# Dividing the feed-forward part between two neighbours

## The chip, the core and the metric

The kernel runs on one core of a Trainium2 chip, as one program. The time is device microseconds of one execution; the program takes 11845.06 us (median of 3 runs, 11842.54 to 11851.63). A core has five engines with instruction streams of their own: PE (TensorE, matmul), DVE (VectorE), ACT (ScalarE), POOL (GpSimd) and SP, which in this kernel issues all the transfers. Each executes its instructions in order; semaphores tie them together. Sixteen DMA engines move the data between HBM and the on-chip SBUF; matmuls write to PSUM, which has 8 banks of 128 x 512 float32.

## The reference

The input `x` is (8, 96, 64, 64). Layer 0 is a selective-scan block with a convolution, layer 1 attention without softmax and a feed-forward part with quantized products:

```python
xz = layernorm(group_norm(x)) @ in_proj_w.T + in_proj_b
xi, z = split(xz, 2)                       # 192 channels each
xi = silu(depthwise_conv3x3(xi) + conv_b)
xs = stack([xi by rows, xi by columns, both reversed])       # K = 4 directions, L = 4096
dts, Bs, Cs = split(einsum('bkdl,kcd->bkcl', xs, x_proj_w), [6, 22])
delta = softplus(einsum('bkrl,kdr->bkdl', dts, dt_proj_w) + dt_proj_b)
h[t] = exp(delta[t] * A) * h[t-1] + (delta[t] * u[t]) * B[t];  y[t] = h[t] . C[t]
y = layernorm(sum of the 4 directions + D * u) * silu(z)
x = x + y @ out_proj_w.T + out_proj_b
t = tokens(x)
t = t + linear_attention(layernorm(t))     # 6 heads, no softmax
t = t + ffn(layernorm(t))                  # 96 -> 384 -> 96
# ffn: operands rounded to 8 bits (5 exponent, 2 mantissa), sums to 16 bits, relu between
```

## The kernel before, in words

Two images form a pair; a loop runs over four pairs, and once more for the end of the last. Tensors are laid out with channels on the partitions and 512 positions (`F`) in a row, so an image has 8 chunks (`NCH`). For one pair the loop body does:

1. `back` of the pair before (sum of the directions, normalization, output projection, keys and values of the attention) together with `project` of the new pair (normalizations, input projection into the padded tiles `ybuf`).
2. `tail` of the pair before, the feed-forward part, together with `convolve` of the new pair.
3. `gates`: Silu over the three tiles `xi`, on ACT, 24 instructions (L354).
4. `prepare`: the scan's inputs.
5. `scan`: all four directions of the pair, in an order written out by hand.

`tail` works on 16 items, an item being a chunk of one image. An item is a generator of three parts: loads of `tf` (L830) and `ta` (L832), the attention's product `pa` (L834), the sum `t2` on DVE (L836), and the function `norm`: `ncp` on PE (L670), its square `nsq` on ACT (L672), `nvp` on PE (L674), Ln and Exp on ACT (`nrs`, L189 and L190), the product `tq` on DVE (L677); then three matmuls `pf1` (L843) with ACT and DVE behind each (`h16` and `hq`, L845 to L847); then three `pf2` (L851), `y16` on ACT and DVE (L855, L856), the sum `ot` on POOL (L858) and its store (L859). One step of the generator `tail` starts an item and advances the two items before it by a part, so 16 items take 18 steps.

`convolve` does 9 taps for the tiles 0 and 2 of `xi` on DVE (L342, L344) and those of tile 1 on PE (`pc`, L328), in 19 steps. `together(one, other, n, m)` lets the program text alternate: for each of `n` steps of `one` so many steps of `other` that `m` are reached at the end, and then the rest of both.

`prepare` loops over 2 orders of the positions, 8 chunks and 2 directions, 32 rounds. A round projects `xi` to `pt` (L392, PE), copies it to `S` (L396, ACT), stores B and C of it (`bs`, `cs`, L398), and for each of three tiles T: `pq` on PE (L404), Softplus to `delta` on ACT (L408), `du` on DVE (L412), and `delta` split into three bfloat16 parts `dp`, by ACT (L424), DVE (`rest`, L425), ACT (L426) and POOL (L427). Then `du` and `dp` are stored (L359, L362), `dp` to `dl`. In the second order POOL first copies three transposed tiles (`u`, L384). The tiles `S`, `delta`, `du` and `dp` have 3 buffers each.

Except in `scan`, the instructions of all engines are put in order by a scheduler of the framework, which takes a neighbour's instruction forward when it estimates that the one due still waits; transfers go through one queue, SP's. A transfer waits, by the built order, for the one eight before it. The ACT tables are in sets: Ln and Exp in one, Silu and Softplus in others. The function `table` keeps the instructions that need one in program order and loads the set with Ln and Exp where it is due (L180); the loads of the other sets are put in by the compiler.

Of the kernel before, what the change touches and what calls it, by code (L numbers as in the profile page):

```python
# [16 lines left out]
PSUM = bass.MemoryType.PSUM  # L17
# [34 lines left out]
def vss_attn_ffn(ctx: ExitStack, tc: tile.TileContext, a: dict):  # L52
# [119 lines left out]
    def half(T):  # L172
        return 1 if T == 2 else 0
# [188 lines left out]
                nc.sync.dma_start(dst(DI * b + 128, 64), src[64 * b : 64 * b + 64])  # L362


    def prepare(xi, us, dl, du, bs, cs_):
        with ExitStack() as st:
            tmp = st.enter_context(tc.tile_pool(name="p2", bufs=3))
            ps = st.enter_context(tc.tile_pool(name="p2ps", bufs=3, space=PSUM))
            pd = st.enter_context(tc.tile_pool(name="p2pd", bufs=4, space=PSUM))

            for T in range(3):
                spread(lambda o, n: us[o : o + n], T, xi[T])
# [2 lines left out]
            for o in range(2):  # L375
                for c in range(NCH):
                    cs = bass.ts(c, F)
# [11 lines left out]
                    for k in (o, o + 2):  # L389
                        pt = ps.tile([128, F], F32, name="pt")  # L390
                        for T in range(3):
                            nc.tensor.matmul(  # L392
                                pt[:76], xw[:, k, T], u[T], start=(T == 0), stop=(T == 2)
                            )
                        S = tmp.tile([128, F], F32, name="S")
                        nc.scalar.activation(S[:76], pt[:76], AF.Copy)  # L396
                        for v, r in ((bs, 0), (cs_, 32)):
                            nc.sync.dma_start(  # L398
                                v[k, 2 * c : 2 * c + 2].rearrange("j p t -> p j t"),
                                S[r : r + 32].rearrange("p (j t) -> p j t", j=2),  # L400
                            )
                        for T in range(3):
                            pq = pd.tile([128, F], F32, name="pq")
                            nc.tensor.matmul(  # L404
                                pq, dtw[64:76, k, T], S[64:76], start=True, stop=True
                            )
                            d = tmp.tile([128, F], F32, name="delta")
                            table("softplus", lambda: nc.scalar.activation(  # L408
                                d, pq, AF.Softplus, bias=dtb[:, k, half(T) : half(T) + 1]
                            ))  # L410
                            q = tmp.tile([128, F], F32, name="du")
                            nc.vector.tensor_tensor(q, d, u[T], ALU.mult)  # L412
                            j = slice(c * F // TC, (c + 1) * F // TC)
                            spread(
                                lambda o, n: duv[k, j, o : o + n].rearrange("j p t -> p j t"),
                                T, q.rearrange("p (j t) -> p j t", t=TC),
                            )

                            dp = tmp.tile([128, F // TC, 3, TC], BF16, name="dp")
                            rest = tmp.tile([128, F], F32, name="rest")  # L420
                            d, rest = [
                                t.rearrange("p (j t) -> p j t", t=TC) for t in (d, rest)
                            ]
                            nc.scalar.activation(dp[:, :, 0], d, AF.Copy)  # L424
                            nc.vector.tensor_tensor(rest, d, dp[:, :, 0], ALU.subtract)  # L425
                            nc.scalar.activation(dp[:, :, 1], rest, AF.Copy)  # L426
                            nc.gpsimd.tensor_tensor(dp[:, :, 2], rest, dp[:, :, 1], ALU.subtract)  # L427
                            spread(
                                lambda o, n: dlv[k, j, :, o : o + n]
                                .rearrange("j a p t -> p (j a) t"),  # L430
                                T, dp.rearrange("p j a t -> p (j a) t"),
                            )


    def scan(dl, du, bs, cs_, ys):
# [431 lines left out]
                going = [g for g in going if next(g, 0) is None]  # L867
                yield

    def together(one, other, n, m):  # L870

        done = 0
        for i in range(n):
            next(one, None)
            while done * n < (i + 1) * m:
                next(other, None)
                done += 1
        for g in (one, other):
            for _ in g:
                pass  # L880

    old = {}
    for pair in range(npair + 1):

        new = {}
# [9 lines left out]
        none = iter(())  # L895
        with ExitStack() as pads, ExitStack() as xis:
            if new:

                yp = pads.enter_context(tc.tile_pool(name="yp", bufs=1, side="right"))
                ybuf = [yp.tile([128, (HH + 2) ** 2], F32, name=f"y{T}") for T in range(3)]  # L900
            with ExitStack() as st:
                def pool(name, bufs, **kw):
                    return st.enter_context(tc.tile_pool(name=name, bufs=bufs, **kw))
                one = other = none
                if old:
                    one = back(
                        pair - 1, old["ys"], old["us"], old["zs"], old["t1"], old["tn"],
                        pool("bk", 2), pool("bky", 1, space=PSUM), pool("bkc", 2, space=PSUM),
                        pool("bkm", 1, space=PSUM), pool("bkp", 2, space=PSUM),
                    )  # L910
                if new:
                    other = project(
                        pair, new["zs"], ybuf, pool("p1", 1, side="right"),
                        pool("p1t", 2, side="right"), pool("p1ps", 2 if old else 6, space=PSUM),
                    )
                together(one, other, 16 if old else 1, 34)
            if pair == 0:
                decay_weights()
            if new:
                xp = xis.enter_context(tc.tile_pool(name="xip", bufs=1))  # L920
                xi = [xp.tile([128, L], F32, name=f"xi{T}") for T in range(3)]
            with ExitStack() as st:
                one = other = none
                if old:
                    one = tail(
                        pair - 1, old["t1"], old["tn"], pool("tt", 3), pool("tps", 6, space=PSUM)
                    )
                if new:
                    other = convolve(
                        xi, ybuf, pool("p1c", 1, side="right"), pool("p1cp", 2, space=PSUM)  # L930
                    )
                together(one, other, 18 if old else 1, 19)
            pads.close()
            if new:
                gates(xi)
                prepare(xi, new["us"], new["dl"], new["du"], new["bs"], new["cs"])
        if new:
            scan(new["dl"], new["du"], new["bs"], new["cs"], new["ys"])
        old = new
# [114 lines left out]
```

## Time and profile before

| what | value |
|---|---|
| median of 3 runs | 11845.06 us |
| the profiled execution, its own time | 11820.4 us |
| its span, first to last instruction | 11818.4 us |
| mean granted PE clock | 0.816 |
| busiest engine, DVE | 8756.4 us, 74% |
| bytes moved | 2092.92 MB, mean 177 GB/s |
| `tail` and `convolve` together, second pair | 2980 to about 3162 us |
| gates, second pair | 3162.3 to 3179.9 us |
| `prepare`, second pair, first `delta` to last `dp` | 3182.6 to 3503 us |
| `tail` alone, after the last pair | 11636 to 11818 us |

Times in the profile are microseconds from the first instruction. A group is an engine's instructions of one line; `out<-in` are the tiles by their names in the program. A window gives each engine's busy time between two moments. In a timeline, the bracket behind an instruction is the idle time of its engine just before it and what ended it. The granted clock is the share of PE's full clock. Busy time of PE is modelled from pipelined matmuls.

### The profile page before, as it was taken

The page shows a single profiled execution, that of the slowest core. Times are in us where ns is not written, and L with a number is a line of the kernel's source. Part 1 is how long each engine was busy: PE and PEld are TensorE (multiplying, and loading weights), DVE is VectorE, ACT ScalarE, POOL GpSimd, SP SyncE. Part 2 cuts the span into 40 slices and gives each one's busy share as a digit, 9 for nine tenths or more (in the row PEclk, how much of TensorE's full clock was granted, in tenths as well). Part 3 has the DMA queues.
Part 4 walks back from the last instruction along what each step waited for, and adds up shares of the span by engine and source line. Part 5 has one row for each costly group of instructions (what it writes and reads, how often), then busy time and mean ns, then how long its engine had stood idle before and what let it go on. Part 6 is the DMA issues. An engine that isn't in the chain of part 4 may idle for free. (4 is left out here: it accounts for less than half of the span.)

```text
span 11818.4 us, 387513 instructions
## 1 busy us (share of the span) xinstructions
PE 8675.0 (73%) x170112; PEld 5662.7 (48%) x170112; DVE 8756.4 (74%) x6465; ACT 6900.1 (58%) x12176; POOL 7986.7 (68%) x2770
## 2 busy tenths in 40 slices
PE   7856666779877666667986666667898666667787
PEld 2245555544225555554422555555442355555542
DVE  5489999963549999995355999999454699999922
ACT  3556666644456666664455666666445566666623
POOL 0489999960249999994025999999313699999910
PEclk8678888879768888888976888888896788888896
DMA  2988888875398888886459888888646988888862
GB/s 79 215 198 201 198 203 201 198 160 134 97 215 195 203 201 200 204 195 149 120 125 209 197 202 199 197 199 199 148 99 156 203 199 199 200 198 200 193 132 63
DMA packets 1655919, 2092.92 MB, mean 177 GB/s; under 512 B 962179, under 2 KB 1307348, under 8 KB 1651412
## 3 DMA queue, kind: packets, MB, share of 16 engines
q1 hardware_dynamic: 1654228, 2068.13, 75.4%
q8 instruction: 1335, 21.87, 0.9%
q14 instruction: 356, 2.92, 0.1%
HBM read 1604.17 MB, written 463.54 MB: 175 GB/s over the span
## 5 line engine op out<-in xcount | busy, mean ns | idle before, releaser
L588 DVE TENSOR_TENSOR_SCAN h<-da,dbu 128x774 f32<-128x774 f32 x4096 | 7028.4, 1760 | 646.5 <-ACT da L577 443.1
L552 POOL TENSOR_TENSOR dbu<-dut,bc 128x1536 f32<-128x1536 f32 x2048 | 7083.1, 3506 | 578.1 <-ACT dbu L549 478.7
L577 ACT ACTIVATE da<-da 128x768 f32<-128x768 f32 x4092 | 3254.2, 797 | 2155.9 <-PE da L570 2117.6
L606 PE MATMUL yp<-h,cw 128*32 128x48 f32 x131072 | 3145.2, 246 | 1126.0 <-issue 1110.7
L570 PE MATMUL da<-dm,aw 128*128 128x128 bf16 x24576 | 2502.0, 251 | 1447.2 <-DVE h L588 1098.1
L606 PEld LDWEIGHTS yp<-h,cw 128*32 128x32 f32 x131072 | 2548.9, 155 | 1673.2 <-issue 1408.7
L570 PEld LDWEIGHTS <-aw 128*128 128x128 bf16 x24576 | 1844.5, 111 | 1774.5 <-issue 1452.5
L506 ACT ACTIVATE cw<-bc,blk 128x512 f32<-128x512 f32 x2048 | 1472.8, 720 | 297.9 <-DMA bc<-cs 216.2
L745 POOL TENSOR_TENSOR yk<-yk 128x768 f32<-128x768 f32 x64 | 115.8, 1809 | 1268.2 <-DMA yk<-ys 1010.6
L427 POOL TENSOR_TENSOR dp<-rest,dp 128x512 bf16<-128x512 f32 x384 | 458.1, 1194 | 707.3 <-ACT dp L426 691.6
L425 DVE TENSOR_TENSOR rest<-delta,dp 128x512 f32<-128x512 f32 x384 | 301.1, 785 | 628.2 <-ACT dp L424 628.2
L404 PE MATMUL pq<-S,dtw 12*128 12x512 f32 x768 | 594.8, 882 | 140.2 <-ACT delta L408 75.3
L614 ACT ACTIVATE yev<-yp 128x384 f32<-128x384 f32 x1024 | 503.4, 492 | 243.1 <-PE yp L606 240.6
L858 POOL TENSOR_TENSOR ot<-t,y 96x512 f32<-96x512 f32 x64 | 128.1, 2002 | 612.0 <-DVE y L856 593.7
L786 DVE SCALAR_TENSOR_TENSOR g<-yc,c_onw,yrs 96x512 f32<-96x512 f32 x128 | 89.9, 742 | 483.2 <-ACT yrs L190 483.2
L404 PEld LDWEIGHTS pq<-S,dtw 12*128 12x128 f32 x768 | 162.4, 250 | 566.0 <-ACT delta L408 179.1
L426 ACT ACTIVATE dp<-rest 128x512 bf16<-128x512 f32 x384 | 241.6, 630 | 327.3 <-DVE rest L425 327.3
L672 ACT ACTIVATE nsq<-ncp 96x512 f32<-96x512 f32 x128 | 75.8, 592 | 572.8 <-PE ncp L670 559.6
L549 ACT COPY dbu<-h 128x12 f32<-128x12 f32 x1984 | 407.1, 205 | 0.0
L758 PEld LDWEIGHTS py<-ident,yk 128*24 128x24 f32 x8192 | 231.6, 108 | 241.7 <-issue 182.6
L758 PE MATMUL py<-ident,yk 128*24 128x128 f32 x8192 | 319.1, 290 | 31.5 <-DVE yk L744 25.7
L384 POOL COPY u<-xi 128x512 f32<-128x512 f32 x96 | 109.3, 1156 | 327.6 <-ACT xi L354 296.6
(136 smaller groups left out, 6684.3 us busy)
## 6 DMA issues: line engine op xcount, KB each, us to landing
dut<-du SPq DMA_DIRECT2D x1024, 768.0 KB
dm<-dl SPq DMA_DIRECT2D x512, 576.0 KB
dl<-dp SPq DMA_DIRECT2D x256, 384.0 KB
dm<-dl SPq DMA_DIRECT2D x512, 192.0 KB
ys<-yev SPq DMA_DIRECT2D x1024, 96.0 KB
du<-du SPq DMA_DIRECT2D x256, 256.0 KB
bc<-bs SPq DMA_DIRECT2D x512, 128.0 KB
bc<-cs SPq DMA_DIRECT2D x512, 128.0 KB
```

Of the source, the lines that this page charges most:

```text
L404: nc.tensor.matmul(pq, dtw[64:76, k, T], S[64:76], start=True, stop=True)
L425: nc.vector.tensor_tensor(rest, d, dp[:, :, 0], ALU.subtract)
L427: nc.gpsimd.tensor_tensor(dp[:, :, 2], rest, dp[:, :, 1], ALU.subtract)
L506: nc.scalar.activation(cw[i % 2][:, :, :, m, :].rearrange("p z j t -> p (z j) t"), bc[i][:, 1].rearrange("p z (j t) -> p (z j) t", j=NB), ...
L549: nc.scalar.copy(start, segs(hs[s - 1][:, :, r])[:, :, :, 1 if back else TC])
L552: nc.gpsimd.tensor_tensor(segs(t)[:, :, :, 1:], dut[g // 2][:, NI * (r % 2) : NI * (r % 2) + NI, :].unsqueeze(1) .to_broadcast([128, 2, NI ...
L570: nc.tensor.matmul(e[:, i], aw[k, r][:, i, z, :], dm[s][:, NI * r + i, :], start=True, stop=True,)
L577: nc.scalar.activation(e, e, AF.Exp)
L588: nc.vector.tensor_tensor_scan(hs[s][:, w, r][:, d], da[p % 3][:, o : o + W6][:, d], dbu[4 * s + r][:, w][:, d], 0.0, ALU.mult, ALU.add,)
L606: nc.tensor.matmul(y[32 * q : 32 * q + 32, 2 * NE * i : 2 * NE * i + 2 * NE] .rearrange("p (j r i) -> p i j r", j=2, r=NR), w[:, z, :, t], ...
L614: nc.scalar.activation(yev[s][:, :, o : o + 8, :].rearrange("p j i e -> p i j e"), y[:, 0 : 16 * NE].rearrange("p (i j e) -> p i j e", j=2 ...
L758: nc.tensor.matmul(o, yk[:, k, 4 * g + e, NE * j : NE * j + NE], ident, start=False, stop=(k + j == 4),)
```

## The change

`together` gets an argument `rest`: with False it stops after `n` steps of `one` and only finishes `other`. `prepare` becomes a generator that yields after each of its 32 rounds. Feed-forward steps 1 to 7 stay beside the 19 steps of the convolution; then the padded tiles are given back and the gates follow; the other 11 steps alternate with the first 24 rounds of `prepare`, and its last 8 rounds follow. The PSUM banks are divided anew: `tail` has 4 (8 after the last pair) where it had 6, `pt` 2 where it had 3, `pq` 2 where it had 4 (4 in the first pair, which has no `tail` beside it).

```diff
-    def prepare(xi, us, dl, du, bs, cs_):
+    def prepare(beside, xi, us, dl, du, bs, cs_):
         with ExitStack() as st:
             tmp = st.enter_context(tc.tile_pool(name="p2", bufs=3))
-            ps = st.enter_context(tc.tile_pool(name="p2ps", bufs=3, space=PSUM))
-            pd = st.enter_context(tc.tile_pool(name="p2pd", bufs=4, space=PSUM))
+            ps = st.enter_context(tc.tile_pool(name="p2ps", bufs=2, space=PSUM))
+            pd = st.enter_context(tc.tile_pool(name="p2pd", bufs=2 if beside else 4, space=PSUM))
...
                                 T, dp.rearrange("p j a t -> p (j a) t"),
                             )
+                        yield
...
-    def together(one, other, n, m):
+    def together(one, other, n, m, rest=True):
...
-        for g in (one, other):
+        for g in (one, other) if rest else (other,):
             for _ in g:
                 pass
...
                     one = tail(
-                        pair - 1, old["t1"], old["tn"], pool("tt", 3), pool("tps", 6, space=PSUM)
+                        pair - 1, old["t1"], old["tn"],
+                        st.enter_context(tc.tile_pool(name="tt", bufs=3)),
+                        st.enter_context(tc.tile_pool(name="tps", bufs=4 if new else 8, space=PSUM)),
                     )
                 if new:
-                    other = convolve(
-                        xi, ybuf, pool("p1c", 1, side="right"), pool("p1cp", 2, space=PSUM)
-                    )
-                together(one, other, 18 if old else 1, 19)
-            pads.close()
-            if new:
-                gates(xi)
-                prepare(xi, new["us"], new["dl"], new["du"], new["bs"], new["cs"])
+
+                    with ExitStack() as sc:
+                        other = convolve(
+                            xi, ybuf, sc.enter_context(tc.tile_pool(name="p1c", bufs=1, side="right")),
+                            sc.enter_context(tc.tile_pool(name="p1cp", bufs=2, space=PSUM)),
+                        )
+                        together(one, other, 7, 19, rest=False)
+                    pads.close()
+                    gates(xi)
+                    other = prepare(
+                        bool(old), xi, new["us"], new["dl"], new["du"], new["bs"], new["cs"]
+                    )
+                together(one, other if new else none, 11 if old else 1, 24)
```

## The prediction

> **What bounds the kernel now.** I read the page first, then the stretch between two scans in windows, then the chain inside two of these windows, then the transfers. No engine is full over the span:
>
> ```profile
> PE 8675.0 (73%) x170112; PEld 5662.7 (48%) x170112; DVE 8756.4 (74%) x6465; ACT 6900.1 (58%) x12176; POOL 7986.7 (68%) x2770
> ```
>
> The change leaves the scans alone, so the stretch between two of them is what counts. The windows, for the second pair of images (columns: window, its length, PE, PEld, DVE, ACT, POOL busy with instruction counts, granted clock, DMA share, GB/s):
>
> ```profile
> 2980.00:3099.00 119.00, 103.05 (x247) 39.93 (x245) 116.05 (x121) 44.62 (x77) 31.60 (x13) 0.92 0.20 58
> 3099.00:3162.00 63.00, 46.61 (x68) 13.07 (x68) 22.25 (x53) 22.51 (x39) 6.67 (x6) 0.53 0.12 35
> 3162.00:3183.00 21.00, 14.87 (x30) 4.77 (x30) 3.03 (x9) 20.78 (x35) 6.43 (x7) 0.82 0.25 94
> 3183.00:3343.00 160.00, 155.21 (x199) 40.29 (x198) 64.72 (x95) 95.01 (x160) 57.72 (x49) 0.61 1.00 228
> 3343.00:3502.00 159.00, 116.89 (x164) 30.92 (x162) 78.47 (x102) 92.93 (x159) 77.35 (x67) 0.67 0.98 215
> ```
>
> Four stages stand there. Convolution beside the feed-forward part is bound by DVE (116 of 119 us). Then 63 us of feed-forward alone, with no engine full and the DMA at 0.12. Then the gates on ACT (20.78 of 21). Then `prepare`, 319 us, bound by the DMA (1.00 and 0.98). The third and fourth pairs show the same lengths within 3 us. The 63 us are a chain, one step of 10.9 us after the other, as ACT in the timeline shows (start, length, what, idle time before it and who ended it):
>
> ```profile
> 3147.72 0.59 ACT L672 ACTIVATE nsq<-ncp 96x512 f32<-96x512 f32 x1 [3.90 <-PE ncp L670]
> 3150.43 0.68 ACT L189 ACTIVATE nrs<-nvp,eps 96x512 f32<-96x512 f32 x1 [2.11 <-PE nvp L674]
> 3151.14 0.63 ACT L190 ACTIVATE nrs<-nrs 96x512 f32<-96x512 f32 x1
> 3151.76 0.59 ACT L855 ACTIVATE y<-pf 96x512 f16<-96x512 f32 x1
> 3152.96 1.58 ACT L845 ACTIVATE h<-pf 128x512 f16<-128x512 f32 x3 [0.60 <-PE pf L843]
> ```
>
> In `prepare` ACT runs one third of a (direction, chunk) round about every 3.3 us (320 us for 96 of them):
>
> ```profile
> 3234.26 0.63 ACT L424 ACTIVATE dp<-delta 128x512 bf16<-128x512 f32 x1 [0.20 <-DMA dl<-dp]
> 3235.65 0.63 ACT L426 ACTIVATE dp<-rest 128x512 bf16<-128x512 f32 x1 [0.76 <-DVE rest L425]
> 3236.18 0.67 ACT L408 ACTIVATE delta<-pq,c_dtb 128x512 f32<-128x512 f32 x1
> ```
>
> The first of the three waits for a store to land and free a buffer, so the DMA paces it. Two more rows: the transfers of 3200 to 3400, and PE inside `prepare`.
>
> ```profile
> q1 hardware_dynamic: 134826, 43.95, 100.5%
> ```
>
> ```profile
> 3250.00:3350.00 100.00, 100.00 (x119) 26.15 (x119) 41.96 (x63) 62.37 (x105) 36.70 (x32) 0.55 1.01 220
> ```
>
> The DMA is full at 220 GB/s, and PE shows busy throughout as well, but at a clock of 0.55.
>
> **The gain: 71 us in each of three pairs.** In the changed kernel's built order of DVE (a list without times) only feed-forward items 0 to 6 lie among the convolution's instructions. Before, a DVE period is 10.94 us (the `y` starts at 3060.54 and 3071.49), of which three convolution passes of 2.27 are 6.8, so an item costs 4.13. The convolution alone is 32 x 2.27 + 5.6 (four first passes) = 78.2; seven items add 29. So it ends at 2980 + 107 = 3087, against 3098.9 before, and the gates no longer wait for the rest of the feed-forward part. 16 to 17 us of gates remain behind it, to 3104; then ACT does item 7's `nsq`, waits for its `nvp` (2.0), does Ln and Exp (1.3) and loads the table of Softplus (1.3): about 7 us. First `delta` at 3111 instead of 3182.6. Bounds: 60, if the convolution ends no earlier than before (3098.9 + 17 + 7 = 3123), and 76, if item 7 hides under the gates. I take 71, the counted order.
>
> **What `prepare` pays.** Nine whole items (7 to 15) and the end of item 6 move in.
>
> DMA: in the built order of SP five `ta` loads, four `tf` loads and ten `out` stores now stand among `prepare`'s transfers, 19 x 192 KB = 3.74 MB; the other loads go ahead of it. At 220 GB/s that is 17 us; at the rate of the feed-forward part (9.05 MB took 16.9% of 182 us) 12.7. DMA is the bound here, so nothing hides it: 15.
>
> ACT: the order gives one feed-forward step per 24/11 rounds, 6.5 thirds, 21.8 us at today's pace. ACT needs at least 1.39 + 0.53 + 0.57 + 0.2 (its share of `S`) = 2.7 a third, 17.6 in all. A step adds nsq 0.59, Ln 0.68, Exp 0.63, three h 1.57, y 0.59 = 4.1 and two table loads, of which the order has 17 more per pair:
>
> ```profile
> 3162.33 1.28 ACT L354 ACT_TABLE_LOAD   x1
> 3163.63 0.72 ACT L354 ACTIVATE xi<-xi,c_convb 128x512 f32<-128x512 f32 x1
> ```
>
> From load to next instruction 1.30. Sum 17.6 + 4.1 + 2.6 = 24.3, less some 1.5 that fall into the 0.76 waits for `rest`: 22.8, against 23.2 that the DMA now needs (21.8 + 15/11). ACT is 98% full, so each wait of a feed-forward instruction costs. In the chain above ACT waits 3.90 + 2.11 + 0.60 = 6.6 a step for PE. If all showed, nine items cost 59; none, if `prepare`'s matmuls that the order puts between always cover them. I take 25: three instructions of `prepare` stand between most of these links, but not all.
>
> The Trainium skill ("ScalarE: Activation LUTs", What ACT_TABLE_LOAD costs, and its rules) speaks against this edit: finish one table set before switching, at about 2.66 us a switch, a drain included. The row above shows 1.3 and no drain. By the page the 17 switches are 45 us instead of 22 and ACT, not the DMA, would be the bound, with a sum about 23 us a pair worse.
>
> SP: `prepare`'s stores keep their order but for two places, where 14 and 7 small transfers stand in a row, among them `tf` loads that wait for PE's `pa` and a `ta` load that waits for DVE's `t2`; the stores `du` and `dl` queue behind, and with them `dp` buffers and ACT. Bounds 0 and one round of stores each (10.4, what ACT waited once for a `cs` store): 0 to 21. I take 2, since in the built order a transfer waits only for the one eight before it, so several are always under way. None of these edits can gain, as the DMA is full before.
>
> DVE gets 9 x 4.1 = 37 on 143 of 319 us, POOL nine `ot` at 1.15 to 3.14, so 10 to 28 on 135: both have room. An `ot` that waits for `y` holds the `dp` queued behind it; that is in ACT's bounds. PSUM: the feed-forward part has 4 banks instead of 6, `pq` 2 instead of 4, `pt` 2 instead of 3. Two `pq` are 6.6 us of ACT's pace, and the first stage is bound by DVE: 0, with ACT's 59 as cover for more. In the first pair only `pt` changes, 0 to 5 us. The last pair has 8 banks, but its order on PE, DVE and ACT is that of before: 0.
>
> **Sum.** 71 - 15 - 25 - 2 = 29 a pair, 87 in three. The profiled execution took 11820.4 (span 11818.4): 11733. The median is 24.7 above it: 11845 - 87 = 11758.
>
> **Rivals.**
> *It is hidden whole.* Only the transfers are paid: 71 - 17 = 54 a pair, 162 in all, 11683. For it: ACT, DVE and POOL are 59%, 45% and 42% busy in `prepare`. Against it: ACT's in-order sum above.
>
> *PE becomes the bound (slower).* At the low clock `pt` and `pq` take 0.925 us a record (3.70 for 4), 11.1 a round, which is more than the 10 us the DMA gives it; an item adds 1.91 + 1.99 + 2.02 + 1.44 + 1.49 = 8.9 (`pa`, `ncp`, `nvp`, `pf` twice, from the last pair, where the clock is 0.50), nine 80. Up to 3422, where the feed-forward part ends, PE has about 26 us left: 54, with the waits of 25 79, and if the waits also use up the slack 105. It turns slower at 71. Worst: 3 x (105 - 71) = 102, 11947. For it: 100 us at full occupancy without a rise of the clock. Against: the clock was 1.00 while the convolution ran beside the same items, and it reaches 0.86 for a few us whenever PE lags. The skill ("TensorE: Matmul & The Clock Gate", Part 1) says a window of 3.4 us without idling gives the full clock; by it this rival falls, since PE would need half the time. The row at 0.55 contradicts it.
>
> *No difference.* Costs of 63 to 79 a pair leave 11821 to 11869.
>
> **How the numbers follow.** Under 0.2% (24 us) this kernel's measurement can hardly be told from no change. Forecast (costs 25 to 63 a pair, 11707 to 11821): 0.50. Hidden: 0.15. No difference: 0.10. Slower, mostly by PE: 0.25. So faster 0.65, same 0.10, slower 0.25. The range leaves out a twentieth below the hidden case and some 0.15 above: 11675 to 11910; the faster cases alone span 11675 to 11821.
>
> **What the profile would show.** Right: the gates start near 3088 and the first `delta` near 3111; the window of feed-forward alone is gone; `prepare` lasts 355 to 365 us, DMA at 0.90 or more; ACT 250 us busy in it with 17 more table loads. Hidden: 335 us, DMA 0.98. PE: a clock near 0.5 with PE busy all through and the DMA under 0.85, `prepare` above 390. Wrong in the first step: the convolution ends after 3099.

## The result, and the profile after

The changed kernel takes 11842.4 us (median of 20 runs, 11819.98 to 11890.16), the kernel before on the same chip 11843.8 us (20 runs, 11793.85 to 11881.49). The ratio is 1.0008 with a 95% interval of 0.9996 to 1.0019: no difference that can be measured. 87 us of gain were forecast.

The two profiled executions have spans of 11818.4 and 11851.0 us. The stretches between two scans are 36 us longer in the second, all the rest 4 us shorter. The interval of the 20 runs leaves room for some 22 us of loss only, so a part of the 36 belongs to these two executions or is made up where these stretches do not show it; which, is not known. I cut the stretches by single instructions: the convolution's first tap, the table load ahead of the first `delta`, the end of the last `dp`, the scan's first instruction (us, for the three pairs that have a feed-forward part beside them):

| | before | after | forecast |
|---|---|---|---|
| convolution | 118.8, 118.3, 118.8 | 102.4, 102.4, 102.6 | 107 |
| first tap to first `delta`'s table | 201.2, 201.7, 201.3 | 118.6, 118.7, 118.8 | 71 less |
| `prepare` | 320.7, 321.6, 324.1 | 420.4, 420.3, 420.4 | 42 more |
| last `dp` to scan | 31.6, 31.8, 32.2 | 28.6, 28.3, 28.4 | the same |
| whole stretch | 553.5, 555.1, 557.6 | 567.6, 567.3, 567.6 | 29 less |

So the beginning gained more than forecast, 83 us a pair, and `prepare` lost 98 instead of 42. The first line of the page, and the windows of the second pair (columns as before: PE, PEld, DVE, ACT, POOL busy, granted clock, DMA share, GB/s), for convolution, gates and three parts of `prepare`:

```profile
PE 8636.7 (73%) x170112; PEld 5659.1 (48%) x170112; DVE 8794.6 (74%) x6465; ACT 6951.4 (59%) x12227; POOL 7975.4 (67%) x2770
```

```profile
2981.00:3084.00 103.00, 97.76 (x231) 39.77 (x231) 101.92 (x93) 35.48 (x61) 17.55 (x9) 0.93 0.17 50
3084.00:3100.00 16.00, 9.34 (x17) 2.94 (x16) 3.72 (x9) 15.94 (x28) 6.02 (x6) 0.82 0.38 152
3101.00:3261.00 160.00, 132.33 (x210) 37.87 (x209) 68.59 (x111) 94.67 (x155) 48.17 (x38) 0.71 0.78 179
3261.00:3390.00 129.00, 99.18 (x155) 27.89 (x153) 61.23 (x91) 76.84 (x129) 46.45 (x39) 0.70 0.73 160
3390.00:3521.00 131.00, 90.56 (x112) 22.32 (x112) 66.83 (x77) 67.61 (x115) 64.64 (x51) 0.60 0.88 195
```

The stage of feed-forward alone (63 us at a DMA share of 0.12) is gone. But `prepare` lost its bound: the DMA, 1.00 before, is at 0.78 and 0.73 while items run, and no other engine took its place. ACT is busy 59% of these 289 us, DVE 45%, POOL 33%. The transfers of 3200 to 3400, and PE in the window in which it was full before:

```profile
q1 hardware_dynamic: 93267, 33.00, 74.5%
```

```profile
3250.00:3350.00 100.00, 78.97 (x129) 22.42 (x128) 49.45 (x78) 64.33 (x106) 36.57 (x30) 0.74 0.81 176
```

33.0 MB where there were 43.95. PE stands at 79 of 100 us at a clock of 0.74, up from 0.55: the rival with PE as the bound wanted the opposite, a low clock with PE full. What is there instead is waiting. ACT, across the largest hole (start, length, what, the idle time before it and its releaser):

```profile
3220.66 0.63 ACT L426 ACTIVATE dp<-rest 128x512 bf16<-128x512 f32 x1 [0.76 <-DVE rest L425]
3221.19 0.57 ACT L396 ACTIVATE S<-pt 76x512 f32<-76x512 f32 x1
3233.31 0.59 ACT L673 ACTIVATE nsq<-ncp 96x512 f32<-96x512 f32 x1 [11.54 <-PE ncp L671]
3236.01 0.68 ACT L189 ACTIVATE nrs<-nvp,eps 96x512 f32<-96x512 f32 x1 [2.11 <-PE nvp L675]
```

The lines of DVE and SP for the same moment:

```profile
3219.93 0.69 DVE L425 TENSOR_TENSOR rest<-delta,dp 128x512 f32<-128x512 f32 x1 [1.81 <-ACT dp L424]
3230.51 0.68 DVE L837 TENSOR_TENSOR t<-ta,pa 96x512 f32<-96x512 f32 x1 [9.89 <-DMA ta<-t]
```

```profile
3224.33 1.44 SPq L362 DMA_DIRECT2D dl<-dp  x2
3225.82 0.85 SPq L860 DMA_DIRECT2D out_dram<-ot  x1
3226.72 0.93 SPq L833 DMA_DIRECT2D ta<-t  x1
...
3233.52 0.38 SPq L831 DMA_DIRECT2D tf<-tn  x1
3240.11 0.98 SPq L359 DMA_DIRECT2D du<-du  x2
```

Read from the last fence up: the load of `ta` stands in SP's queue behind the stores of a round, and is issued at 3226.72. `t2` on DVE (L837) waits 9.89 us for it; `ncp`, `nsq` and all that stands behind them on ACT and DVE wait too, though it belongs to `prepare`; so from 3225.8 to 3240.1 no `du` or `dl` is issued, and the DMA has little to move. The waits of ACT over 3101 to 3390 (sum, times, longest) say how much of this there is:

```profile
ACT dp L426 <- DVE rest L425: 40.4, 42, 1.8
ACT nsq L673 <- PE ncp L671: 30.0, 5, 11.5
ACT y L856 <- PE pf L852: 17.5, 6, 4.5
ACT delta L408 <- PE pq L404: 8.9, 11, 2.7
```

One loss in `prepare` has nothing to do with the feed-forward steps. Two memsets of the scan's tile `cw`, 6.9 us each, have moved. In the kernel before, both follow the last `dp` of `prepare`:

```profile
3501.98 1.15 POOL L427 TENSOR_TENSOR dp<-rest,dp 128x512 bf16<-128x512 f32 x1 [1.29 <-ACT dp L426]
3510.49 6.88 DVE L451 MEMSET cw<- 128x8192 f32 x1 [9.25 <-issue]
```

In the changed kernel, and in every run below that has feed-forward steps beside `prepare`, the one on POOL starts 13 to 54 us before the end of the last `dp`, and the one on DVE stands ahead of a late `rest` (here the last one), for which ACT waits:

```profile
3512.51 6.88 DVE L452 MEMSET cw<- 128x8192 f32 x1 [1.66 <-issue]
3519.32 0.62 DVE L425 TENSOR_TENSOR rest<-delta,dp 128x512 f32<-128x512 f32 x1
3519.98 0.63 ACT L426 ACTIVATE dp<-rest 128x512 bf16<-128x512 f32 x1 [8.39 <-DVE rest L425]
```

So the last round of `prepare` takes 17.3 us on ACT instead of 10.0, in all three pairs; of these 7 us only some 3 come back between the last `dp` and the scan. What the memset on POOL costs is not to be read from the trace, and no run moved either back.

### The profile page after: what moved, and what is told of

It reads as the page before. It is cut to its first block, busy times and chain, and to the rows that moved or that the text cites. A ratio compares the mean times of both kernels' runs of the same rounds, so it can differ in the third digit from the quotient of the medians.

```text
span 11851.0 us, 387228 instructions
## 1 busy us (share of the span) xinstructions
PE 8636.7 (73%) x170112; PEld 5659.1 (48%) x170112; DVE 8794.6 (74%) x6465; ACT 6951.4 (59%) x12227; POOL 7975.4 (67%) x2770
## 5 line engine op out<-in xcount | busy, mean ns | idle before, releaser
L859 POOL TENSOR_TENSOR ot<-t,y 96x512 f32<-96x512 f32 x64 | 100.6, 1572 | 523.9 <-DVE y L857 443.9
L550 ACT COPY dbu<-h 128x12 f32<-128x12 f32 x1984 | 407.3, 205 | 0.0
L384 POOL COPY u<-xi 128x512 f32<-128x512 f32 x96 | 112.1, 1182 | 332.7 <-ACT xi L354 298.0
```

The lines of the kernel that those rows point to most:

```text
L550: nc.scalar.copy(start, segs(hs[s - 1][:, :, r])[:, :, :, 1 if back else TC])
```

## The experiments

Each is told with the length of its `prepare` (before: mean 322.1, after: 420.4). Ratios are to the kernel before on the same chip. Runs without an interval are single executions and are read by their stages.

**First: four suspected costs, one by one.**

The loads ahead:

```diff
-            tns = [tmp.tile([DIM + 1, F], F32, name=f"tf{i}", bufs=1) for i in range(4)]
+            tns = [tmp.tile([DIM + 1, F], F32, name=f"tf{i}", bufs=1) for i in range(10)]
-                ta = tmp.tile([DIM, F], F32, name="ta")
+                ta = tmp.tile([DIM, F], F32, name="ta", bufs=10)
```

> The changed kernel with 10 buffers each for `ta` and `tf` instead of 3 and 4, so that all loads of the feed-forward part are issued before the stores of `prepare`; SP then has a regular order. Theory of the late loads: two holes in the DMA of `prepare` (from 3225 and from 3347 us, about 20 us each) vanish and `prepare` shrinks from 420 to about 380 us per pair, the whole kernel to about 11725. Theory of the in-order ACT (table loads and waits for PE): `prepare` stays above 410 and the kernel within 30 us of the changed one. Theory of the banks: no change either.

`prepare` 400.4, 395.2, 395.0: 23.5 us less, 11805.8 us, ratio 0.9957 (0.9943 to 0.9971), 0.4% faster than the kernel before. The late loads were a real cost, more than ten times what the forecast had. But 75 us remain.

No switches of tables (Ln and Exp of the feed-forward part replaced by Copy, so its outputs are not the reference's):

```diff
-        rsqrt(rs, vp[:DIM])
+        nc.scalar.activation(rs, vp[:DIM], AF.Copy)
+        nc.scalar.activation(rs, rs, AF.Copy)
```

> The changed kernel, with Ln and Exp of the feed-forward part replaced by two copies on ACT (its normalization is left out, so the output differs); no table switch is left in `prepare`, and the order of the table instructions is free there. Theory of the tables: the 18 loads of 1.28 us in `prepare` cost 23 us or more, so `prepare` falls from 420 to 395 or less. Theory of the late loads: ACT is not what fills the stage, `prepare` falls by less than 10, the two holes stay.

404.5, 403.6, 401.4: 17.2 us less. That is no clean price of the switches: without the order that the tables impose, the scheduler also put the items elsewhere (in the second pair no item's `nsq` stands between 3144 and 3237 us), and the late loads are still there. The Trainium skill ("ScalarE: Activation LUTs", What ACT_TABLE_LOAD costs) has about 2.66 us a switch, a drain of about 1.38 included, which would be 45 us for 17. In the rows of this case the load takes 1.28 us, the next instruction starts 1.30 us after it does, and no drain shows.

Fewer PSUM banks alone, in the kernel before (`pt` 2, `pq` 2):

```diff
-            ps = st.enter_context(tc.tile_pool(name="p2ps", bufs=3, space=PSUM))
-            pd = st.enter_context(tc.tile_pool(name="p2pd", bufs=4, space=PSUM))
+            ps = st.enter_context(tc.tile_pool(name="p2ps", bufs=2, space=PSUM))
+            pd = st.enter_context(tc.tile_pool(name="p2pd", bufs=2, space=PSUM))
```

> The kernel before with the PSUM banks of `prepare` cut as in the change (`pt` 2 instead of 3, `pq` 2 instead of 4), nothing moved. Theory of the banks: a good part of the 100 us shows here, `prepare` goes from 321 to over 340 us. The two other theories: 321 to 326, as the stores pace it.

330.2, 328.7, 332.7: 8.4 us, with nothing beside it.

Ten steps beside the convolution and eight beside `prepare`:

```diff
-                        together(one, other, 7, 19, rest=False)
+                        together(one, other, 10, 19, rest=False)
-                together(one, other if new else none, 11 if old else 1, 24)
+                together(one, other if new else none, 8 if old else 1, 24)
```

> The changed kernel with 10 feed-forward steps beside the convolution and 8 beside `prepare` (24 of its rounds, as before). The convolution stage grows by three items of 4.1 us, 102 to about 115. If each moved item costs the same (100 us over nine items, 11 each), `prepare` falls by 33 to about 387. If the late loads cost most: the order of SP has one irregular place left instead of two, so `prepare` falls by about 20 for it plus some 5 an item, to about 385; the two are told apart by where the DMA has holes. The kernel gains about 20 us a pair on the changed one, 11780.

378.7, 378.3, 378.4, 42 us less; but the convolution takes 115.3 and the first `delta` comes 29 us later, for the feed-forward items run on beyond the gates. Stretches of 554 to 555, ratio 0.9993 (0.9979 to 1.0006): again no difference.

**Then: what are the 75 us with the loads ahead?** All that follows has the ten buffers, except one control in the kernel before. The rest beside `prepare`, in the run with the loads ahead, is a regular period: the loads of the table for Ln come at 3174.86, 3200.93, 3227.91 and 3255.07, 26 to 27 us a step, where the forecast had 23. ACT in one of them, some lines left out:

```profile
3200.93 1.28 ACT L180 ACT_TABLE_LOAD   x1
...
3210.88 0.59 ACT L846 ACTIVATE h<-pf 128x512 f16<-128x512 f32 x1
3211.36 0.58 ACT L673 ACTIVATE nsq<-ncp 96x512 f32<-96x512 f32 x1
3215.12 0.59 ACT L856 ACTIVATE y<-pf 96x512 f16<-96x512 f32 x1 [3.18 <-PE pf L852]
3215.61 0.62 ACT L424 ACTIVATE dp<-delta 128x512 bf16<-128x512 f32 x1
3217.91 0.63 ACT L426 ACTIVATE dp<-rest 128x512 bf16<-128x512 f32 x1 [1.68 <-DVE rest L425]
```

`y` waits for `pf`, which waits for the `h` just done, and the `delta` that would give PE its next bank stands behind. Over 230 us of this, the window (as above) and ACT's waits:

```profile
3115.00:3345.00 230.00, 189.35 (x314) 54.05 (x312) 109.20 (x173) 146.27 (x240) 75.45 (x61) 0.74 0.77 168
```

```profile
ACT dp L426 <- DVE rest L425: 39.4, 44, 1.7
ACT y L856 <- PE pf L852: 25.8, 8, 4.5
ACT delta L408 <- PE pq L404: 7.5, 7, 2.7
```

146 us of work and, with the shorter ones, 83 of waits: ACT never stands free, but a third of its time is waiting in order.

The eleven steps over all 32 rounds (`together(..., 11, 32)` in place of 24):

> The kernel after with ten buffers each for `ta` and `tf` (as in the run with the loads ahead), and the eleven feed-forward steps beside `prepare` spread over all 32 rounds instead of the first 24. In the run with the loads ahead `prepare` lasted 395 to 400 us with a period of 26.0 us a step of 24/11 rounds while items ran. Theory A (the in-order queue of ACT is too full over the 24 rounds and has slack over the last 8): a step then has 2.9 rounds, so ACT's own work per step is about 32 us at the pace of 10 us a round less the overlap, the DMA becomes the pace again, and `prepare` falls to 375 us or less; the time falls by 45 us or more against the run with the loads ahead, to about 11760. Theory B (each feed-forward step costs a fixed amount, through its table switch and the waits around it, however far apart the steps stand): `prepare` stays at 390 to 400 us, the time within 20 us of 11806.

392.0, 393.1, 392.0, not 375: theory B, as far as `prepare` goes (the one execution took 11778.7 us, 27 under 11806, where theory B allowed 20). With a third more rounds between them, eleven steps cost nearly the same. Where they cost it can be read round by round, from ACT's last `dp` of one round to that of the next (second pair, rounds 4 to 26): every third round takes 13.9 to 17.6 us and the two between 8.0 to 11.7, where the kernel before takes 8.6 to 12.1, mostly 9.4 to 10.5. A step is paid in the round in which it stands, some 6 us, and the rounds behind it do not win it back.

The `out` stores of items 6 to 15 cut to one column:

```diff
-                nc.sync.dma_start(out[2 * pair + b, :, cs], ot)
+                if pair < npair - 1 and 2 * c + b > 5:
+                    nc.sync.dma_start(out[2 * pair + b, :, c * F : c * F + 1], ot[:, 0:1])
```

> The kernel after with ten buffers each for `ta` and `tf`, and in the first three pairs the `out` stores of items 6 to 15 (those beside `prepare`) cut to one of their 512 columns: these outputs are left mostly unwritten, the number of transfers stays. 10 x 192 KB less in each `prepare`. Theory A (DMA bytes are paid in full, as the prediction's DMA term had it): at 220 GB/s 8.9 us a pair, `prepare` 386 to 392 us, about 27 us less in all, near 11780. Theory B (with the in-order waits on ACT as the pace, the DMA has slack and bytes are free): `prepare` 394 to 400 us, the time within 10 us of 11806. Between 3 and 7 us a pair: both in part.

397.3, 393.0, 396.4: 1.3 us less on average, within what the pairs differ. Bytes cost next to nothing here.

Ten and eight steps, with the loads ahead (the edit as above):

> The kernel after with ten buffers each for `ta` and `tf`, and the division at 10 and 8 steps instead of 7 and 11. With late loads this division took 12.9 us more in the convolution and gave first `delta` 39 us later, and `prepare` was 42 us shorter: 554 us a pair against 567. With the loads ahead 7 and 11 gave 542. If the loads were most of the loss in `prepare` at 7 and 11, eight steps now cost 8/11 of what remains: `prepare` 372 to 378 us, a pair 548 to 553, slower than 7 and 11 with the loads ahead by 20 to 30 us (11825 to 11840). If what remains is fixed waits of a step (about 7 us each) instead, three steps fewer give 21 us and cost 39: the same sign, 11850 or more. If the division is better now, under 11800.

377.9, 368.1, 364.8, stretches 553.6, 544.4, 541.3 against 542 to 548; ratio 0.9952 (0.9933 to 0.9970), 11836.1 us. It is no worse than seven and eleven, which I had not expected.

Two items in each step, four double steps and five:

```diff
-                yield
+                if i % 2:
+                    yield
-                        together(one, other, 7, 19, rest=False)
+                        together(one, other, 4, 19, rest=False)
-                together(one, other if new else none, 11 if old else 1, 24)
+                together(one, other if new else none, 5 if old else 1, 24)
```

> The kernel after with ten buffers each for `ta` and `tf`, and two items taken in each step: four double steps beside the convolution and five beside `prepare`, so that two items share one switch of ACT's tables. Inside each `prepare` four loads of Softplus's table fewer than nine and as many of Ln and Exp fewer. Theory A (the switch and the waits around it are a fixed price per step): five steps of double work save some 9 x 1.3 = 12 us of table loads and about four of the chains' waits at 3 to 7 us, `prepare` 370 to 385 us where the run with the loads ahead had 395 to 400, 11740 to 11780. Theory B (not the switches but ACT's and PE's work itself sets the pace): `prepare` 390 us or more, the time within 20 us of 11806; longer runs of ACT without `prepare`'s work in them may also starve the DMA, then above 11806.

379.6, 386.0, 382.5: 14 us shorter, as four table switches and some waits fewer would give; but convolution and gates take 17 us more until the first `delta`. 11827.6 us, ratio 0.9958 (0.9941 to 0.9976), as with the loads ahead alone.

These runs give a price: what `prepare` has above 322.1, by the steps beside it.

| run | steps | us above | us a step |
|---|---|---|---|
| after | 11 | 98.3 | 8.9 |
| loads ahead | 11 | 74.8 | 6.8 |
| the same over 32 rounds | 11 | 70.3 | 6.4 |
| ten and eight | 8 | 56.4 | 7.0 |
| ten and eight, loads ahead | 8 | 48.2 | 6.0 |
| double steps, loads ahead | 5 | 60.6 | 12.1 |

Some 7 us of each row are DVE's memset for the scan and not the steps, and a double step holds two items. Alone, before, a step took 10.9 us; beside the convolution it takes (102.4 - 78.2) / 7 = 3.5, with the forecast's estimate of 78.2 for the convolution alone. So of the 10.9 us only about a fifth is hidden beside `prepare`, with the loads ahead some 40% (a little more without the memset).

**Which resource is the price?** First ACT's order:

```diff
                             nc.scalar.activation(dp[:, :, 0], d, AF.Copy)
                             nc.vector.tensor_tensor(rest, d, dp[:, :, 0], ALU.subtract)
-                            nc.scalar.activation(dp[:, :, 1], rest, AF.Copy)
...
+                            if late:
+                                late.pop()()
```

> The kernel after with ten buffers each for `ta` and `tf` (its `prepare` lasted 395 to 400 us with the loads ahead), and in `prepare` ACT's second `dp` of each third, with the POOL subtraction and the store behind it, is issued after the next third's `delta` and first `dp` (a fourth `dp` buffer). Same work, another order on ACT. With the loads ahead ACT's 230 us from 3115 to 3345 were about 150 of work and 39.4 of waits of the second `dp` for DVE's `rest` (44 times), 25.8 of `y` for PE's `pf`. Theory A (ACT's queue sets the pace of 26.0 us a step, waits included): without the 39.4 a step takes 21.6 us, under the 21.8 to 23.2 of the DMA, and `prepare` falls by 25 us or more, to 372 or less; the time to about 11730. Theory B (the pace comes from the feed-forward chain over PE, PSUM and DVE, whose links ACT only passes on): the waits for `rest` are replaced by others, `prepare` within 8 us of 397, the time within 20 us of 11806.

394.8, 394.7, 396.6. It tells nothing, since the scheduler put the second `dp` back: ACT does it right behind the first in 73 of 96 thirds (82 with the loads ahead alone), with a `delta` between in 4 (3). ACT in the profile of this run:

```profile
3184.23 0.62 ACT L425 ACTIVATE dp<-delta 128x512 bf16<-128x512 f32 x1
3185.68 0.63 ACT L431 ACTIVATE dp<-rest 128x512 bf16<-128x512 f32 x1 [0.83 <-DVE rest L426]
3186.22 0.67 ACT L409 ACTIVATE delta<-pq,c_dtb 128x512 f32<-128x512 f32 x1
```

The copies of items 6 to 15 out of PSUM by DVE:

```diff
-                    nc.scalar.activation(h16, p1, AF.Copy)
+                    (nc.vector.tensor_copy if 2 * c + b > 5 else scopy)(h16, p1)
-                nc.scalar.activation(y16, p2[:DIM], AF.Copy)
+                (nc.vector.tensor_copy if 2 * c + b > 5 else scopy)(y16, p2[:DIM])
```

> The kernel after with ten buffers each for `ta` and `tf`, and from item 6 on the three `h` and the `y` of an item are copied out of PSUM by DVE instead of ACT. This takes 2.2 us of ACT work and its waits for `pf` (25.8 + 3.5 us in 3115 to 3345, 9 items) out of ACT's queue, and adds 4 instructions an item to DVE, which was busy 30 to 40 of 80 us. Theory A (ACT's queue sets the pace): a step falls from 26.0 by about 5.3 to 20.7, under the DMA's pace, `prepare` falls by 25 us or more, to 372 or less, the time to about 11730. Theory B (the chain over PE and PSUM sets it): `prepare` within 8 us of 397. If it falls by 8 to 25, DVE's in-order waits for `pf` take part of the place, since `rest` and `du` queue behind them.

394.5, 386.2, 386.4: 6, 9 and 9 us less, pair by pair. ACT lost its wait of 25.8 us for `pf` and got others: for `rest` 54.6 instead of 39.4, for `ncp` 28.9 instead of 4.5, because, as I read it, DVE now waits for `pf` (23.4 us) with `rest` behind it.

Both, over 32 rounds:

> The kernel after with ten buffers each for `ta` and `tf`, the second `dp` late, the copies of items 6 to 15 on DVE, and the eleven steps beside `prepare` spread over all 32 rounds. Theory A (ACT's queue was the pace): ACT then has work and waits of about 6 us a round against 10 to 10.5 of the DMA, so the DMA paces `prepare` again: 345 to 360 us where 392 was with the spread alone, a pair 495 to 508 instead of 540, and the time 11640 to 11690, faster than both kernels by 1.3% or more. Theory B: within 8 us a pair of the spread alone, 11750 to 11800.

407.5, 405.3, 407.3, a ratio of 0.9985 (0.9975 to 0.9995): a longer `prepare` than with the copies alone or the spread alone. It is no test of theory A, since here too ACT does the second `dp` right behind the first, in 84 of 96 thirds.

The second `dp` late in the kernel before, the control:

> The kernel before with nothing but the second `dp` late (a fourth `dp` buffer): the control. There the DMA was full in `prepare` (1.00 and 0.98) and ACT had slack, so if the DMA paces it, removing ACT's waits for `rest` brings nothing: `prepare` 318 to 326 us, time within 0.2% of before. If `prepare` falls under 312 us, the order on ACT limited the kernel before as well, and the forecast's reading of that stage was wrong.

324.0, 323.1, 320.3, DMA 1.00 to 1.01. But the edit did not reach ACT here either: the second `dp` stands right behind the first in 92 of 96 thirds (93 before), with 67 waits for `rest` from 3190 to 3420, as many as in the kernel before. So this run does not test whether ACT's order counts there; that the DMA paces that `prepare` rests on its share of 1.00 and on the waits for stores to land. The ratio is 0.9979 (0.9964 to 0.9993); no stage shows where a gain would be, and it is the size that can hardly be told from none.

A third of `pt` (T = 0 alone, so two of three of its products are left out):

```diff
-                        for T in range(3):
+                        for T in range(1 if beside else 3):
```

> The kernel after with ten buffers each for `ta` and `tf`; in the pairs with a feed-forward part beside `prepare`, `pt` is computed from one of its three tiles (T = 0 alone), so two of three `pt` products are left out of the result. The engines' other work and all transfers stay. In the run with the loads ahead a step of 26.7 us had PE busy for 22.5 us, about 9 to 10 of them in `pt` (2.2 rounds of 4.5). If PE's work at its low clock sets the pace, a step falls by 5 to 6 us to the DMA's 23 or less, and `prepare` from 395 to 400 to 370 us or less. If ACT's queue sets it, PE only waits more: `prepare` 385 to 400 us, the time within 20 us of 11806.

400.4, 399.4, 400.0: unchanged. The window to hold against that of the loads ahead:

```profile
3115.00:3345.00 230.00, 180.06 (x230) 47.18 (x229) 110.20 (x174) 147.47 (x241) 76.19 (x62) 0.57 0.75 162
```

84 PE records fewer of 314, and PE is busy 180 us instead of 189, while its clock fell from 0.74 to 0.57 (with a third `pq` bank, the next run, it is 0.74 on the same chip). PE's amount of work isn't the price. But its time hardly changed, so the run does not tell whether PE, at its low clock, holds the others up.

A third bank for `pq` (4 for the feed-forward part, 1 for `pt`):

```diff
-            ps = st.enter_context(tc.tile_pool(name="p2ps", bufs=2, space=PSUM))
-            pd = st.enter_context(tc.tile_pool(name="p2pd", bufs=2 if beside else 4, space=PSUM))
+            ps = st.enter_context(tc.tile_pool(name="p2ps", bufs=1 if beside else 2, space=PSUM))
+            pd = st.enter_context(tc.tile_pool(name="p2pd", bufs=3 if beside else 4, space=PSUM))
```

> The kernel after with ten buffers each for `ta` and `tf`, and PSUM divided as 4 banks for the feed-forward part, 1 for `pt` and 3 for `pq` (it was 4, 2, 2). With the loads ahead PE waited 34 us of 230 for ACT's `delta` to free a `pq` bank, 88 with its weight loads. If the two banks couple PE and ACT and so set the pace, `prepare` falls by 15 us or more to 382 or less. If ACT's queue sets it, the waits of PE move to another bank: `prepare` 390 to 402 us.

398.2, 399.7, 402.6: not the banks of `pq` either.

The second `dp` on DVE:

```diff
-                            nc.scalar.activation(dp[:, :, 1], rest, AF.Copy)
+                            nc.vector.tensor_copy(dp[:, :, 1], rest)
```

> The kernel after with ten buffers each for `ta` and `tf`, and the second `dp` of every third is written by DVE, behind its `rest`, instead of by ACT (in all pairs). ACT then has only `delta` and the first `dp` in a third, and no wait for `rest`: where the other instructions of a step allow, 1.2 us a third instead of 2.5. DVE gets 96 instructions of about 0.68 us, 65 us on 120 to 160 of 320. If ACT's queue sets the pace, a step falls from 26.7 to the DMA's 23 or less, `prepare` to 345 to 370 us, a pair to 495 to 520, the time to 11640 to 11740. If PE at its low clock or the banks set it, `prepare` stays at 385 to 400 us and the time at 11780 to 11810. If DVE takes ACT's place as the queue in order, between these.

404.7, 402.5, 405.1; ratio 0.9984 (0.9972 to 0.9996). The window and ACT's first two waits:

```profile
3115.00:3345.00 230.00, 182.61 (x308) 52.50 (x306) 143.40 (x229) 123.03 (x192) 86.50 (x62) 0.77 0.76 166
```

```profile
ACT delta L408 <- DVE rest L425: 41.5, 32, 1.7
ACT y L856 <- PE pf L852: 26.8, 9, 6.5
```

ACT has 23 us less to do and `prepare` isn't shorter: the 39.4 us in which the second `dp` waited for `rest` are now 41.5 in which `delta` waits for it, to get its buffer back. So it isn't ACT's work alone.

The copies on DVE and the steps over 32 rounds, without the late `dp`:

> The kernel after with ten buffers each for `ta` and `tf`, the copies of items 6 to 15 out of PSUM by DVE, and the eleven steps over all 32 rounds: the two edits that each shortened a pair, to 532 and to 540 us, against 542 with the loads ahead alone. If they add up, a pair takes about 530 us, and the time is 11740 to 11765 against 11845 to 11870 of before. If the steps' waits in order only move from ACT to DVE, as in the run with both and the second `dp` late, 545 us or more and 11800 or more.

391.2, 385.9, 388.7, stretches 538.4, 532.2, 534.2; 11766.3 us, ratio 0.9937 (0.9913 to 0.9961). It is the fastest that was measured with an interval, by 0.6%. The two edits do not add up, though: `prepare` is as long as with the copies alone (mean 388.6 against 389.0). And it is 18 us shorter than in the run with both and the late `dp`, which differs by that edit and its fourth `dp` buffer.

More buffers, so that no `delta` waits for a `rest`:

```diff
-                            d = tmp.tile([128, F], F32, name="delta")
+                            d = tmp.tile([128, F], F32, name="delta", bufs=6)
...
-                            rest = tmp.tile([128, F], F32, name="rest")
+                            rest = tmp.tile([128, F], F32, name="rest", bufs=4)
```

(and 5 for `du` and `dp`).

> The kernel after with ten buffers each for `ta` and `tf`, and more buffers in `prepare`: `delta` 6, `rest` 4, `du` and `dp` 5, where each had 3. Same work, same transfers. In the built order ACT's `delta` then no longer waits for a `rest`, and most of the second `dp` have another instruction of ACT ahead of them while `rest` is made. If the round trips over three buffers set the pace (26 to 27 us a step), a step falls to 24.5 us or less and `prepare` from 395 to 400 to 378 us or less, the time to 11755 or less against 11835 to 11860 of before. If they do not, `prepare` stays at 390 to 402 us and the ratio to before at 0.995 to 0.997, as with the loads ahead alone; then the pace is left open.

426.2, 427.6, 441.6: 35 us longer, 11915.0 us, ratio 1.0044 (1.0026 to 1.0063), slower than before. ACT's first two waits:

```profile
ACT delta L408 <- PE pq L404: 46.7, 34, 4.5
ACT dp L426 <- DVE rest L425: 23.1, 26, 1.7
```

The wait for `rest` fell by 16 us, as meant, and `delta` now waits 46.7 for `pq` where it waited 7.5. With more buffers the scheduler built another order: ACT does a `delta` between the two `dp` in 34 of 96 thirds, where it did in 3, and `pq` still has two banks. More buffers together with more `pq` banks were not run. The same buffers beside the two edits that helped gave a ratio of 1.0050 (1.0032 to 1.0069), `prepare` 421 to 427.

What is shown: with the loads ahead, neither less work on PE, nor less on ACT, nor fewer bytes, nor a third bank of `pq`, nor more buffers, each taken alone, made `prepare` more than 8 us shorter on average. Table switches with the loads ahead were not taken away alone. What was taken away on one queue often came back as a wait on another, and the same work with more buffers, in the order that the scheduler then built, took 35 us longer. PE and ACT wait for each other: of the 41 us in 230 in which PE is idle with the loads ahead, it waits 34.3 for ACT's `delta`. That the order which the scheduler wrote sets the pace is my reading, and it is not shown; PE's time at its low clock is a rival that is left, and the same work in an order written by hand was not run. Which link closes the loop stays open.

## Why the prediction was wrong, step by step

The time lies inside the range, but by luck: the gain came out 12 us larger a pair and the cost 56 us larger. By its size the outcome is the rival "no difference", by its sum it is not. The step that failed is the cost of `prepare`: 98 us where 15, 25 and 2 were added up to 42. Of the 98, 23.5 are shown to be late loads, and 7 are read from the trace as a memset of the scan; the cause of the other 67 or so stays open. Term by term:

- **The gain, 71.** Right in kind, 83 in fact, above the upper bound of 76. An item beside the convolution costs 3.5 us instead of 4.13, and item 7 does hide: the gates' table load comes at 3078.9, 5 us before the convolution ends, and the table load for `delta` starts 4.8 us after the last gate does.
- **DMA, 15.** Failed: "DMA is the bound here, so nothing hides it". It was the bound only before. At a share of 0.78 it has room, and with the loads ahead half of the bytes gone changed 1.3 us.
- **SP, 2 of 0 to 21.** Failed outright: 23.5, beyond its bound. The argument was that a transfer waits only for the one eight before it. It priced the stores behind a late load, but not the instructions behind the one that uses it: `t2` on DVE, 9.89 us, with `rest` and `du` behind it and ACT idle for 11.54.
- **ACT, 25 of 0 to 59.** The step of 22.8 us became 26 to 27. "ACT is 98% full" mixed work with waits: of the 2.7 us a third, 0.76 was the wait for `rest`, a trip to DVE and back. I took it as a cover for 1.5 us of other work. In fact it grows to 1.68 (3217.91 above) where `rest` on DVE takes 1.61 us instead of 0.69, beside the feed-forward part's `ot` on POOL. The table loads, 1.3 each, were right.
- **DVE and POOL, 0.** Failed for the same reason: both have room (45% and 33%), yet in order room doesn't help. Moving copies from ACT to DVE moved the waits along. Nor did the sum have a term for the memset on DVE, which costs `prepare` 7 us in its last round.
- **PSUM, 0.** 8.4 us in the kernel before, where the DMA paces it; with the loads ahead a third `pq` bank brought nothing.
- **PE as the bound.** It did not come as forecast: the clock is 0.70 to 0.71 and PE busy 80% while items run. Two thirds of `pt` removed changed nothing, but hardly changed PE's time either.

The forecast's common fault: it mostly compared sums of work per engine, the largest being the pace. With two programs woven into the same five queues, a step cost 8.9 us of the 10.9 that its chain of waits takes alone. That it is this chain that is paid, less what happens to fit under it, is how I read it.

## What to carry to other kernels

Work put beside a stage that looks half idle does not cost its share of the busiest engine. Price it by its chain: every link that waits holds up all that is queued behind it on that engine, and the first thing to take away is a late load (here ten buffers, 0.4%). Where a scheduler writes the order, look at the built order after each edit; it can undo an edit, answer more buffers with a worse order, or move the next stage's memset in front of the last work of this one.

## What the runs showed of the hardware

PE's busy share is no measure of its reserve. With two thirds of `pt` taken away, PE's records fell from 314 to 230 in 230 us, its busy time only from 189 to 180 us, and its granted clock from 0.74 to 0.57: the clock went down with the work, and what was left took nearly as long as before.

An instruction of POOL slows one of DVE. In the run with the loads ahead POOL's sum `ot`, and on DVE the `rest` beside it and one that POOL leaves alone:

```profile
3270.42 1.15 POOL L859 TENSOR_TENSOR ot<-t,y 96x512 f32<-96x512 f32 x1 [4.65 <-DVE y L857]
```

```profile
3270.51 1.61 DVE L425 TENSOR_TENSOR rest<-delta,dp 128x512 f32<-128x512 f32 x1 [0.17 <-ACT dp L424]
3274.39 0.69 DVE L425 TENSOR_TENSOR rest<-delta,dp 128x512 f32<-128x512 f32 x1 [1.67 <-ACT dp L424]
```

The same instruction takes 0.69 us with POOL idle and 1.61 when it begins beside POOL's 1.15. In that `prepare` all six `rest` that an `ot` overlaps take 1.51 to 1.61 us, and all 52 that POOL does not touch 0.62 to 0.69. The Trainium skill ("GPSIMD Engine Reference", 1. Specifications) says that POOL shares its SBUF interfaces with VectorE, and that instructions of DVE with two SBUF inputs, as this one, contend for them. The forecast had put DVE and POOL at nothing without looking at it; 1.61 less 0.69, so 0.9 us a step, is by my estimate the most that it adds to the price.
